# Causal attention layers: the scores of the first two query tiles in one step and one bank a head, and GpSimd's subtractions issued later

## The chip, the cores and the metric

The kernel runs on one core of a Trainium2 chip. The core has TensorE (PE in the profile; its weight loads are PEld), VectorE (DVE), ScalarE (ACT), GpSimd (POOL) and SyncE (SP), each with its own queue of instructions. The metric is the time of the whole program on the device in microseconds; lower is better.

## What is computed

Four layers work on x of shape (4, 512, 128) in float32: half a feed-forward part, attention, half a feed-forward part, each with a layer norm ahead and a residual. The change concerns the attention of layers 0 and 1, which are causal, with 16 heads of 8 values, 4 batches and 512 tokens. Cut to that:

```python
# layer 0, x normed
att = jnp.einsum('bhtd,bhsd->bhts', q, k) / np.sqrt(D) + bias      # bias: a table by head and distance
att = jnp.where(pos[None, :] > pos[:, None], -jnp.inf, att)
x = x + (softmax(att) @ v) @ proj_w.T + proj_b
# layer 1, x normed
logits = einsum(q1, k1) * einsum(q2, k2) * SCALE                   # ranks 4 and 8 a head
logits = jnp.where(causal, -jnp.inf, logits)
x = x + (softmax(logits) @ v) @ Wo.T + bo
```

The attention of layer 3 isn't causal and takes another branch of the same function; layer 2 has a recurrence instead.

## The kernel before

`attention()` (L566) serves layers 0, 1 and 3. A unit is one batch and one group of four heads, so a layer has 16 units. Queries are cut into four tiles of 128 rows, i = 0 to 3; tile i sees (i + 1) x 128 keys. The argument `added` (a table for layer 0, a mask for layer 1) selects the causal branch. Its names in the profile are `s_a` (scores), `sc_a` and `top_a` (scores with the addend, and each row's largest), `t_a` (transposed), `w_a` (weights by key), `acc_a` (their products with the values), `ou_a`, `ot_a`, `otok_a`, `oT_a` and `proj_a` (the output's way out).

For tile i of unit u the work is:

- `scores(u, i)`: TensorE makes four products, one a head, each in a PSUM bank of its own (L587). VectorE reduces them in the order of heads 2, 0, 3, 1: it adds the table or mask, writes the sum to SBUF and finds the row's largest (L604 for heads 0 and 1, L608 for 2 and 3). For heads 0 and 1 GpSimd subtracts the largest (L605), issued at once. For heads 2 and 3 ScalarE will take the exponential with the largest as its bias; this is kept in the list `put_off`.
- `exponentials()`: issues what is in `put_off` (L617) and empties it.
- `weights(u, i)`: TensorE transposes the scores by 128x128 blocks into banks (L628). ScalarE takes them out, with an exponential for heads 0 and 1 (L637) and a plain copy for heads 2 and 3 (L639).
- `values_up_to(u, i)`: TensorE multiplies by the padded values, all tiles and heads of a unit in one bank (L650). Behind tile 3, ScalarE copies the bank out (`summed`, L734).

The order of the instructions is written out by hand: within `manual_schedule` TensorE, VectorE, ScalarE and GpSimd run in the order in which the code issues. Banks come from a pool of eight and are handed on in the order of release, so which engine frees a new bank depends on the order too.

The main loop goes over u, and within u over j = 0 to 3. Each j issues: `weights(u, j)`; `exponentials()`; the values of the tile before (of unit u-1's tile 3 if j is 0); `scores(u + 1, j)`; then parts of other work, a step of the next batch's beginning (`begin_next`, with norm, transposition T_a at L180, then qk, or the factors in layer 1, and the values) or a step of what follows a finished batch (`go_on`). At j = 0 it also issues `start(u + 2)`: the unit's q on ScalarE in layer 0 (L911), q on VectorE and k on GpSimd in layer 1 (L1183), and two units into a batch the projection of the batch before (`ended`, L762). At j = 2 the unit before is normalized (`ot_a`, L741). A batch's norm has two steps on GpSimd (rs and rstd, L157 and L158), and its n is made on VectorE (L171) and then transposed and copied to `nT_a` (L127 on VectorE or L129 on ScalarE).

So a unit on TensorE is: t0, values of tile 3 of the unit before, s0, parts; t1, values of tile 0, s1, parts; t2, values of tile 1, s2, ot; t3, values of tile 2, s3. Here ti are the transposes of tile i of unit u and si the scores of tile i of unit u+1.

Of the kernel before, what the change touches and what calls it, by code (L numbers as in the profile page):

```python
# [11 lines left out]
AF = mybir.ActivationFunctionType  # L12
ALU = mybir.AluOpType
# [4 lines left out]
P = 128  # L18
# [3 lines left out]
NT = S // P  # L22
# [5 lines left out]
SLOT = 32  # L28
# [8 lines left out]
HUGE = 3.0e38  # L37
# [4 lines left out]
def kernel(ctx: ExitStack, tc: tile.TileContext, a: dict, out: bass.AP):  # L42
    nc = tc.nc
# [12 lines left out]
    def bank(name):  # L56
        return psum.tile([P, 512], FP, name=name, tag="bank", bufs=8)
# [508 lines left out]
    def attention(pool, tag, begin, project, residual, owT, added, after=None, beside=(), fetch=None):  # L566
# [5 lines left out]
        units = [(b, g) for b in range(NB) for g in range(NG)]  # L572
        st = {}

        def begun(b):
            if ("begin", b) not in st:
                st["begin", b] = begin(b)
            return next(st["begin", b], "end") != "end"

        def start(u):  # L580
            b, g = units[u]
            if g == 0:
                st["o", b] = pool.tile([P, NT, NG, NG * HD], FP, name=f"otok_{tag}{b}", tag="otok")
            st["qk", u] = project(b, g)

        def product(ps, q, k, r, i, n0, n1):
            nc.tensor.matmul(  # L587
                ps[:, n0:n1], q[r : r + SLOT, i * P : (i + 1) * P], k[r : r + SLOT, n0:n1], start=True, stop=True
            )


        def scores(u, i):
            b, g = units[u]
            q, k = st["qk", u]
            n = (i + 1) * P
            banks = [bank(f"s_{tag}{u}_{i}{r}") for r in range(4)]
            for r in range(4):
                product(banks[r], q, k, r * SLOT, i, 0, n)
            for r in (2, 0, 3, 1):
                sc = pool.tile([P, n], FP, name=f"sc_{tag}{u}_{i}{r}", tag=f"sc{i}", bufs=4)  # L600
                top = small.tile([P, 1], FP, name=f"top_{tag}{u}_{i}{r}", tag="top", bufs=16)
                more = added(g * 4 + r)[:, S - n :]
                if r < 2:
                    nc.vector.tensor_tensor_reduce(sc, banks[r][:, :n], more, 1.0, -HUGE, ALU.add, ALU.max, top)  # L604
                    nc.gpsimd.tensor_scalar(sc, sc, top, None, ALU.subtract)  # L605
                else:

                    nc.vector.tensor_tensor_reduce(sc, banks[r][:, :n], more, -1.0, HUGE, ALU.add, ALU.min, top)  # L608
                    put_off.append((sc, top))
                st["sc", u, i, r] = sc  # L610

        put_off = []

        def exponentials():

            for sc, top in put_off:
                nc.scalar.activation(sc, sc, AF.Exp, bias=top, scale=-1.0)  # L617
            put_off.clear()

        def weights(u, i):  # L620

            n = (i + 1) * P
            each = min(4, S // n)
            for r0 in range(0, 4, each):
                ps = bank(f"t_{tag}{u}_{i}{r0}")
                for x in range(each):
                    for j in range(i + 1):
                        nc.tensor.transpose(  # L628
                            ps[:, x * n + j * P : x * n + (j + 1) * P],
                            st["sc", u, i, r0 + x][:, j * P : (j + 1) * P],  # L630
                            ident,
                        )
                w = pool.tile([P, S], FP, name=f"w_{tag}{u}_{i}{r0}", tag="w", bufs=8)

                m = max(0, min(each, 2 - r0)) * n
                if m > 0:
                    nc.scalar.activation(w[:, :m], ps[:, :m], AF.Exp)  # L637
                if m < each * n:
                    nc.scalar.copy(w[:, m : each * n], ps[:, m : each * n])  # L639
                for x in range(each):  # L640
                    st["w", u, i, r0 + x] = w[:, x * n : (x + 1) * n]

        def values_up_to(u, i):

            b, g = units[u]
            if i == 0:
                st["acc", u] = bank(f"acc_{tag}{u}")
            for j in range(i + 1):
                for r in range(4):
                    nc.tensor.matmul(  # L650
                        st["acc", u][r * SLOT : (r + 1) * SLOT, i * P : (i + 1) * P],
                        vpads[b % 2][:, j, g * 4 + r, :],
                        st["w", u, i, r][:, j * P : (j + 1) * P],
                        start=(j == 0),
                        stop=(j == i),
                    )
            if i == NT - 1:
                summed(u)
# [15 lines left out]
        def lowered(u):  # L674
            q, k = st["qk", u]
            ps = bank(f"low_{tag}{u}")
            for i in range(NT):
                nc.tensor.transpose(ps[:, i * P : (i + 1) * P], st["low", u][:, i, :], ident)  # L678
            ql = pool.tile([P, S], FP, name=f"ql_{tag}{u}", tag="ql", bufs=2)
            nc.vector.tensor_tensor(ql, ps, q, ALU.add)  # L680
            st["ql", u] = ql
# [50 lines left out]
        def summed(u):  # L732
            o_u = pool.tile([P, S], FP, name=f"ou_{tag}{u}", tag="ou", bufs=3)
            nc.scalar.copy(o_u, st["acc", u])  # L734
            st["ou", u] = o_u
# [35 lines left out]
        def begin_next(u, between=False):  # L771
# [2 lines left out]
            b = (u + 1) // NG + 1  # L774
            return u % NG not in ((2, 3) if between else (2,)) and b < NB and begun(b)

        n_units = len(units)
        lead = 2 * NT + 2
        padded_values(pool)
# [7 lines left out]
        with tc.manual_schedule(engines={E_.PE, E_.DVE, E_.Activation, E_.Pool}):  # L787
            while begun(0):
                pass
            for u in range(3):  # L790
                if fetch is not None:
                    fetch(*units[u])
                if u > 0:
                    start(u - 1)
            if added:
                for i in range(NT):
                    scores(0, i)
                    exponentials()
            else:

                for n in range(0, lead, 2):
                    if n == 2 * NT:
                        lowered(0)
                    together(step(largest, n), step(largest, n + 1))
            for u in range(n_units + 1):
                last = u - 1
                now, nxt = u < n_units, u + 1 < n_units
                for j in range(NT):
                    n = 2 * (u * NT + j)

                    of = (u, j - 1) if j > 0 and now else (last, NT - 1) if j == 0 and last >= 0 else None
                    if added:
                        if now:
                            weights(u, j)
                        exponentials()

                        if of:
                            values_up_to(*of)
                        if nxt:
                            scores(u + 1, j)  # L820
                        if rest or not begin_next(u, True):
                            go_on()
                    else:
                        together(step(largest, n + lead), step(by_key, n))
                        if of:
                            times_values(*of, 0)
                        if j == NT - 1 and nxt:
                            lowered(u + 1)
                        if rest or not begin_next(u, True):
                            go_on()  # L830
                        together(step(largest, n + 1 + lead), step(by_key, n + 1))
                        if of:
                            times_values(*of, 1)
                    if j == 0 and u + 2 < n_units:
                        start(u + 2)
                    if j == 0 and last >= 1 and units[last - 1][1] == NG - 1:
                        ended(units[last - 1][0])
                    elif not begin_next(u):
                        go_on()
                    if j % 2:  # L840
                        next(beside, None)
                    if j == 2 and last >= 0:
                        normalized(last)
                    if j == 3 and fetch is not None and u + 3 < n_units:
                        fetch(*units[u + 3])
                    if j == 3 and last >= 0 and units[last][1] == NG - 1:
                        gathered(units[last][0])
            ended(NB - 1)
            while rest:
                go_on()  # L850
# [584 lines left out]
    ps = bank("gate0T")  # L1435
# [99 lines left out]
```

## Time and profile before

| | us |
|---|---|
| median of three runs | 1565.0 |
| the runs | 1563.73 to 1570.41 |
| profiled execution | 1562.17 |
| its span, first to last instruction | 1560.5 |
| causal attention of layer 0, about | 127 to 352 |
| causal attention of layer 1, about | 543 to 775 |

The mean granted clock of TensorE is 0.893 of full speed. The page's groups that the change touches (line, engine, operation, count, then busy time and mean ns of one, then the idle time ahead of them and what ended most of it):

```profile
L605 POOL TENSOR_SCALAR sc_a<-sc_a,top_a 128x128 f32<-128x128 f32 (+3 forms) x256 | 275.4, 1091 | 112.1 <-DVE top_a L604 72.2
L587 PE MATMUL s_a<-k_a,q_a 32*128 32x512 f32 (+3 forms) x1536 | 267.1, 549 | 17.9 <-DMA k_a<-fac_a 14.2
L628 PE MATMUL t_a<-ident,sc_a 128*128 128x128 f32 x1280 | 172.3, 282 | 6.0 <-DVE top_a L608 5.6
L617 ACT ACTIVATE sc_a<-sc_a,top_a 128x128 f32<-128x128 f32 (+3 forms) x256 | 135.0, 577 | 23.8 <-DVE top_a L608 23.6
L650 PE MATMUL acc_a<-w_a,vpad 128*32 128x128 f32 x2560 | 98.4, 280 | 0.6 <-DVE top_a L604 0.6
```

The group of L587 holds the products of layer 3 with those of the two causal layers. Busy times of TensorE overlap, since its matmuls are pipelined; for what a group costs in a row of groups, the distance from its start to the next group's start is the better measure.

### The profile page before, as it was taken

To read this page: it belongs to the slowest core of one execution; us is meant where nothing else is said; L and a number is where in the kernel's file an instruction comes from. 1 tells how busy PE (TensorE), PEld (TensorE's weight loads), DVE (VectorE), ACT (ScalarE), POOL (GpSimd) and SP (SyncE) were. 2 spreads that over 40 slices of the span, in tenths; PEclk is the share of its full clock that TensorE was granted. 3 is DMA by queue.
4 is the path that set the end of the run, shared out by engine and by line. 5 is a ranking of instruction groups with operands and counts; after the bars stand their busy time and mean duration, and the time that the engine had idled before them with its cause. 6 is when DMAs were issued, how large, how long until landed. Compare 5 with 4: busy or idle time off the path is not lost. (4 is left out here: it accounts for less than half of the span.)

```text
span 1560.5 us, 28691 instructions
## 1 busy us (share of the span) xinstructions
PE 1264.9 (81%) x10523; PEld 821.3 (53%) x10523; DVE 864.1 (55%) x2947; ACT 712.9 (46%) x1487; POOL 655.7 (42%) x789
## 2 busy tenths in 40 slices
PE   4777998995969688989988676718779999998394
PEld 3455676773756455766756655616533343333273
DVE  5335676773325365766556455515367787774343
ACT  1234876871443165768643322203325655564041
POOL 3455767872520176777501111273632214212253
PEclk9997999996979888999999778758979999999597
DMA  7420240002515474442033302214204000000223
GB/s 231 129 57 8 77 164 12 9 13 64 148 35 109 126 226 123 136 123 69 2 78 116 135 0 109 114 50 114 64 21 171 14 3 13 12 5 15 75 79 105
DMA packets 103092, 123.12 MB, mean 79 GB/s; under 512 B 9404, under 2 KB 74152, under 8 KB 100904
## 3 DMA queue, kind: packets, MB, share of 16 engines
q1 hardware_dynamic: 96296, 108.07, 23.2%
q0 software_dynamic: 6656, 13.22, 2.6%
q8 instruction: 84, 1.38, 0.4%
q14 instruction: 56, 0.46, 0.1%
HBM read 79.27 MB, written 41.98 MB: 78 GB/s over the span
## 5 line engine op out<-in xcount | busy, mean ns | idle before, releaser
L605 POOL TENSOR_SCALAR sc_a<-sc_a,top_a 128x128 f32<-128x128 f32 (+3 forms) x256 | 275.4, 1091 | 112.1 <-DVE top_a L604 72.2
L587 PE MATMUL s_a<-k_a,q_a 32*128 32x512 f32 (+3 forms) x1536 | 267.1, 549 | 17.9 <-DMA k_a<-fac_a 14.2
L692 ACT ACTIVATE w_a<-t_a 128x512 f32<-128x512 f32 x256 | 140.4, 595 | 119.7 <-PE t_a L587 94.8
L628 PE MATMUL t_a<-ident,sc_a 128*128 128x128 f32 x1280 | 172.3, 282 | 6.0 <-DVE top_a L608 5.6
L489 POOL DMA_INDIRECT res_f<-y_f,back_f x112 | 109.7, 980 | 141.8 <-ACT y_f L488 101.3
L587 PE MATMUL t_a<-ql_a,k_a 32*128 32x512 f32 x512 | 168.8, 643 | 0.5 <-DVE low_a__12599 L672 0.2
L628 PEld LDWEIGHTS t_a<-ident,sc_a 128*128 128x128 f32 x1280 | 145.1, 144 | 36.8 <-issue 13.8
L617 ACT ACTIVATE sc_a<-sc_a,top_a 128x128 f32<-128x128 f32 (+3 forms) x256 | 135.0, 577 | 23.8 <-DVE top_a L608 23.6
L587 PEld LDWEIGHTS s_a<-k_a,q_a 32*128 32x128 f32 x1536 | 93.7, 188 | 88.9 <-issue 43.1
L637 ACT ACTIVATE w_a<-t_a 128x256 f32<-128x256 f32 (+2 forms) x192 | 94.2, 526 | 64.2 <-PE t_a L628 63.7
L395 POOL DMA_INDIRECT disp_f<-n_f,to_f x96 | 94.3, 983 | 66.8 <-issue 58.8
L501 PE MATMUL o_f<-w_l,h_f 128*128 128x128 f32 (+1 forms) x896 | 113.0, 279 | 3.8 <-DVE o_f L483 3.3
L501 PEld LDWEIGHTS o_f<-w_l,h_f 128*128 128x128 f32 (+1 forms) x896 | 103.0, 184 | 14.7 <-DVE o_f L483 6.0
L466 PE MATMUL h_f<-dT_f,w_l 128*128 128x320 f32 (+1 forms) x256 | 107.8, 559 | 2.8 <-ACT dT_f L444 2.8
L157 POOL TENSOR_SCALAR rs_f<-mv_f 128x4 f32<-128x4 f32 (+1 forms) x23 | 6.5, 281 | 233.4 <-DVE mv_f L154 232.7
L650 PE MATMUL acc_a<-w_a,vpad 128*32 128x128 f32 x2560 | 98.4, 280 | 0.6 <-DVE top_a L604 0.6
L639 ACT COPY w_a<-t_a 128x256 f32<-128x256 f32 (+2 forms) x192 | 93.7, 528 | 6.7 <-PE t_a L628 6.5
L672 DVE TENSOR_REDUCE low_a__12599<-s_a 128x1 f32<-128x512 f32 x128 | 82.1, 685 | 26.3 <-PE t_a L587 18.5
L608 DVE CUSTOM_DVE_ANT_0 sc_a<-s_a,future 128x128 f32<-128x128 f32 (+3 forms) x128 | 62.3, 487 | 57.2 <-PE s_a L587 44.2
L672 DVE TENSOR_REDUCE low_a__12597<-s_a 128x1 f32<-128x512 f32 x128 | 81.3, 683 | 20.5 <-PE t_a L587 15.1
L608 DVE CUSTOM_DVE_ANT_0 sc_a<-s_a,table 128x128 f32<-128x128 f32 (+3 forms) x128 | 62.4, 487 | 53.0 <-PE s_a L587 52.5
L488 ACT ACTIVATE y_f<-o_f,d_f 128x128 f32<-128x128 f32 (+1 forms) x112 | 38.8, 394 | 105.9 <-DVE o_f L483 102.3
(337 smaller groups left out, 2260.8 us busy)
## 6 DMA issues: line engine op xcount, KB each, us to landing
gb_f<-rows_f SPq DMA_DIRECT2D x16, 1024.0 KB
fac_a<-fac_a_sb SPq DMA_DIRECT2D x36, 256.0 KB
disp_f<-zeros_f SPq DMA_DIRECT2D x4, 2080.0 KB
d_f<-disp_f SPq DMA_DIRECT2D x32, 260.0 KB
w_l<-in_L_ffn_w_dram SPq DMA_DIRECT2D x16, 512.0 KB
cb_f<-rows_f SPq DMA_DIRECT2D x16, 512.0 KB
q_a<-fac_a SPq DMA_DIRECT2D x32, 256.0 KB
k_a<-fac_a SPq DMA_DIRECT2D x32, 256.0 KB
```

Source lines behind the costliest of these rows:

```text
L395: nc.gpsimd.indirect_dma_start(out=self.to[c][i0 + t][:, :], out_offset=bass.IndirectOffsetOnAxis(ap=to[:, c, t : t + 1], axis=0), in_=ns[ ...
L466: nc.tensor.matmul(ps[u][:, :cap], w1[:, e, (c + u) * P : (c + u + 1) * P], dT, start=True, stop=True)
L489: nc.gpsimd.indirect_dma_start(out=self.back[e * per + s][:, :], out_offset=bass.IndirectOffsetOnAxis(ap=back[:m, s : s + 1], axis=0), in_ ...
L501: nc.tensor.matmul(po[:m, s, :], h[:, c, s * P : s * P + m], w2[:, e, c, :], start=(c == 0), stop=(c == NC - 1),)
L587: nc.tensor.matmul(ps[:, n0:n1], q[r : r + SLOT, i * P : (i + 1) * P], k[r : r + SLOT, n0:n1], start=True, stop=True)
L605: nc.gpsimd.tensor_scalar(sc, sc, top, None, ALU.subtract)
L608: nc.vector.tensor_tensor_reduce(sc, banks[r][:, :n], more, -1.0, HUGE, ALU.add, ALU.min, top)
L617: nc.scalar.activation(sc, sc, AF.Exp, bias=top, scale=-1.0)
L628: nc.tensor.transpose(ps[:, x * n + j * P : x * n + (j + 1) * P], st["sc", u, i, r0 + x][:, j * P : (j + 1) * P], ident,)
L650: nc.tensor.matmul(st["acc", u][r * SLOT : (r + 1) * SLOT, i * P : (i + 1) * P], vpads[b % 2][:, j, g * 4 + r, :], st["w", u, i, r][:, j * ...
L672: nc.vector.tensor_reduce(st["low", u][:, i, c : c + 1], ps, AX.X, ALU.max, negate=True)
L692: nc.scalar.activation(w, ps, AF.Exp)
```

## The change

`scores()` takes a tuple of tiles. A head's bank holds the scores of all tiles of the tuple side by side: for (0, 1), tile 0 in columns 0 to 127 and tile 1 in 128 to 383. All products of the tuple are issued first, then the reductions tile by tile, which are now in `larger()`. The main loop takes the tiles in steps (0, 1), (2,) and (3,), each at the j of its first tile: at j = 0 the weights of tiles 0 and 1, the values of the unit before's tile 3, and the scores of tiles 0 and 1; at j = 1 nothing of these; at j = 2 the weights of tile 2, the values of tiles 0 and 1 and the scores of tile 2; j = 3 as before. Parts, `start(u + 2)`, the projection and the normalization keep their j.

GpSimd's subtractions go into `put_off` with the exponentials, and both are issued by the next `exponentials()`, which runs at each j. Those of tiles 0 and 1 are so issued at j = 1, behind the parts and `start(u + 2)` of j = 0; those of tile 2 at j = 3, behind the parts of j = 2; those of tile 3 at the next unit's j = 0, behind its transposes' issue and the parts of j = 3. The exponentials of tile 0 move from the start of j = 1 to the same place with tile 1's behind them, and tile 1's move ahead from j = 2 to j = 1. The number of instructions of each kind and shape stays.

```diff
-        def scores(u, i):
+        def scores(u, tiles):
+
             b, g = units[u]
             q, k = st["qk", u]
+            banks = [bank(f"s_{tag}{u}_{tiles[0]}{r}") for r in range(4)]
+            at = {i: sum((x + 1) * P for x in tiles if x < i) for i in tiles}
+            for i in tiles:
+                for r in range(4):
+                    product(banks[r][:, at[i] :], q, k, r * SLOT, i, 0, (i + 1) * P)
+            for i in tiles:
+                larger(u, i, [ps[:, at[i] : at[i] + (i + 1) * P] for ps in banks])
+
+        def larger(u, i, banks):
+            b, g = units[u]
             n = (i + 1) * P
-            banks = [bank(f"s_{tag}{u}_{i}{r}") for r in range(4)]
-            for r in range(4):
-                product(banks[r], q, k, r * SLOT, i, 0, n)
             for r in (2, 0, 3, 1):
...
                 if r < 2:
-                    nc.vector.tensor_tensor_reduce(sc, banks[r][:, :n], more, 1.0, -HUGE, ALU.add, ALU.max, top)
+                    nc.vector.tensor_tensor_reduce(sc, banks[r], more, 1.0, -HUGE, ALU.add, ALU.max, top)
+                    put_off.append((sc, top, True))
+                else:
+
+                    nc.vector.tensor_tensor_reduce(sc, banks[r], more, -1.0, HUGE, ALU.add, ALU.min, top)
+                    put_off.append((sc, top, False))
+                st["sc", u, i, r] = sc
+
+        put_off = []
+
+        def exponentials():
+
+
+            for sc, top, less in put_off:
+                if less:
                     nc.gpsimd.tensor_scalar(sc, sc, top, None, ALU.subtract)
                 else:
...
+                    nc.scalar.activation(sc, sc, AF.Exp, bias=top, scale=-1.0)
             put_off.clear()
...
+        steps = ((0, 1), (2,), (3,))
...
-                for i in range(NT):
-                    scores(0, i)
+                for tiles in steps:
+                    scores(0, tiles)
                     exponentials()
...
+                        tiles = next((t for t in steps if t[0] == j), ())
                         if now:
-                            weights(u, j)
+                            for i in tiles:
+                                weights(u, i)
                         exponentials()
 
-                        if of:
-                            values_up_to(*of)
-                        if nxt:
-                            scores(u + 1, j)
+                        for i in steps[steps.index(tiles) - 1] if tiles else ():
+                            if j > 0 and now:
+                                values_up_to(u, i)
+                            elif j == 0 and last >= 0:
+                                values_up_to(last, i)
+                        if nxt and tiles:
+                            scores(u + 1, tiles)
                         if rest or not begin_next(u, True):
                             go_on()
```

More of the change, by code (lines that the diff above doesn't have):

```diff
@@ L603, in scores @@
                 if r < 2:
-                    nc.vector.tensor_tensor_reduce(sc, banks[r][:, :n], more, 1.0, -HUGE, ALU.add, ALU.max, top)
-                    nc.gpsimd.tensor_scalar(sc, sc, top, None, ALU.subtract)
-                else:
-                    nc.vector.tensor_tensor_reduce(sc, banks[r][:, :n], more, -1.0, HUGE, ALU.add, ALU.min, top)
-                    put_off.append((sc, top))
+                    nc.vector.tensor_tensor_reduce(sc, banks[r], more, 1.0, -HUGE, ALU.add, ALU.max, top)
+                    put_off.append((sc, top, True))
+                else:
+                    nc.vector.tensor_tensor_reduce(sc, banks[r], more, -1.0, HUGE, ALU.add, ALU.min, top)
+                    put_off.append((sc, top, False))
                 st["sc", u, i, r] = sc
@@ L614, in exponentials @@
         def exponentials():
-            for sc, top in put_off:
-                nc.scalar.activation(sc, sc, AF.Exp, bias=top, scale=-1.0)
+            for sc, top, less in put_off:
+                if less:
+                    nc.gpsimd.tensor_scalar(sc, sc, top, None, ALU.subtract)
+                else:
+                    nc.scalar.activation(sc, sc, AF.Exp, bias=top, scale=-1.0)
             put_off.clear()
```

## The prediction, made before the changed kernel ran

> **What bounds the kernel now.** I read the page's busy shares first, then the busy time of the engines in stretches of the two causal stages (about 127 to 352 us for L0, 543 to 775 us for L1), then TensorE's waits there, then the order of single groups.
>
> The page, whole program, busy time:
>
> ```profile
> PE 1264.9 (81%) x10523; PEld 821.3 (53%) x10523; DVE 864.1 (55%) x2947; ACT 712.9 (46%) x1487; POOL 655.7 (42%) x789
> ```
>
> The stretches (start:end, length, then busy us of PE, PEld, DVE, ACT, POOL, then the granted clock):
>
> ```profile
> 127.00:180.00 53.00, 47.27 (x544) 33.00 (x544) 34.01 (x155) 37.35 (x81) 36.19 (x36) 0.94 0.11 36
> 180.00:240.00 60.00, 56.67 (x712) 40.41 (x712) 45.77 (x205) 45.90 (x102) 43.27 (x46) 1.00 0.34 126
> 240.00:300.00 60.00, 54.98 (x668) 39.78 (x668) 41.18 (x184) 42.13 (x92) 42.57 (x45) 0.94 0.03 8
> 600.00:660.00 60.00, 57.43 (x730) 39.38 (x729) 42.60 (x181) 43.68 (x96) 44.66 (x42) 0.97 0.39 120
> ```
>
> TensorE is busy 89 to 96%, VectorE, ScalarE and GpSimd each 64 to 77%. So TensorE paces; the other three have 2.6 to 4 us of slack in a unit of 11.5, enough to be late at one place but not to bound the stage. TensorE's waits (total, times, longest), first from 127 to 360 us, then from 540 to 775 us:
>
> ```profile
> PE T_a L180 <- DVE n_a L171: 11.6, 6, 3.4
> PE proj_a L762 <- ACT ou_a L734: 1.6, 2, 0.8
> PE lg_f L322 <- DVE nT_f L127: 0.8, 1, 0.8
> ```
>
> ```profile
> PE s_a L587 <- DMA k_a<-fac_a: 14.2, 1, 14.2
> PE t_a L628 <- DVE top_a L608: 5.6, 5, 4.3
> PE T_a L180 <- DVE n_a L171: 5.4, 3, 3.7
> PE s_a L587 <- ACT w_a L637: 2.4, 1, 2.4
> ```
>
> Waits are few. What can be won is TensorE's own steps, and these few. One plain unit on TensorE (start, length, group):
>
> ```profile
> 164.96 0.66 PE L628 MATMUL t_a<-ident,sc_a 128*128 128x128 f32 x4
> 165.55 1.08 PE L650 MATMUL acc_a<-w_a,vpad 128*32 128x128 f32 x32
> 166.56 0.54 PE L587 MATMUL s_a<-k_a,q_a 32*128 32x128 f32 x8
> 167.02 1.09 PE L628 MATMUL t_a<-ident,sc_a 128*128 128x128 f32 x8
> 168.04 0.43 PE L650 MATMUL acc_a<-w_a,vpad 128*32 128x128 f32 x8
> 168.40 0.76 PE L587 MATMUL s_a<-k_a,q_a 32*128 32x256 f32 x8
> 169.09 1.82 PE L628 MATMUL t_a<-ident,sc_a 128*128 128x128 f32 x12
> 170.84 0.65 PE L650 MATMUL acc_a<-w_a,vpad 128*32 128x128 f32 x16
> 171.41 0.93 PE L587 MATMUL s_a<-k_a,q_a 32*128 32x384 f32 x8
> ```
>
> Start to start: t0 0.59, values of tile 3 1.01, s0 0.46, t1 1.02, values of tile 0 0.36, s1 0.69, t2 1.75, values of tile 1 0.57. With tile 3 behind, the unit ends at 176.47: 11.5 us.
>
> **What the Trainium skill says.** "PSUM — Partial Sum Buffer", section "PSUM bank collisions raise a hardware error": two engines must not touch one bank and quadrant at once, even in other columns, so semaphores guard whole banks. The changed program keeps this: VectorE's first reduction of tile 0 waits for a count that TensorE raises only behind tile 1's product in that bank. No trace here has two tiles in one bank yet. "TensorE: Matmul & The Clock Gate", Part 1, "What's actually happening": after an idle window of about 3.4 us the clock is halved until TensorE was busy about as long. The trace agrees: after waits of 2.77 and 2.13 us at 139 to 145 us the clock of the next 5 us is 0.51 and the sixteen transposes of tile 3 take 3.55 us instead of 1.84. "Trainium Architecture — The Big Picture", "Inside one NeuronCore": each engine works through its own stream and meets the others only at semaphores; hence I follow each engine's order.
>
> **The change part by part.** Counts of instructions are equal; order and banks change. A unit is one batch and four heads; 32 in the two stages, 30 with a next unit's scores.
>
> (1) Merged groups. t0 and t1 1.61 us, as twelve transposes in a row 1.46 (t2 without a wait): I take 1.50. Values of tiles 0 and 1 0.93, as 24 in a row 0.80 (tile 2's step, 174.60 to 175.40): 0.80. s0 and s1 1.15; s2 moves the same columns in half the products in 0.86: 1.00, an estimate between. Sum 0.39; I take 0.35, 30 times: -10.5.
>
> (2) t2's fourth group of transposes now takes the bank of the last unit's values, freed by ScalarE, instead of one freed by VectorE's first reduction of s1. It shows as 1.75 instead of 1.46 three times in L0 and as waits of about 0.2 to 0.4 us in L1, 1.1 together: -2.0.
>
> (3) TensorE comes about 1.5 us later, with more work ahead, to what it waited for in units with extra parts: the projection (step of s0 1.53 instead of 0.45: 1.1, three times: 3.3), router logits (1.0 once, and three s2 of 1.44 instead of 0.86 while ScalarE is late with weights: 2.7), ranks (s1 1.57 instead of 0.67, twice: 1.8). -7.8. Bound from below: nothing goes where the part's own chain moves along too.
>
> (4) Differences behind parts. GpSimd (0.61, 0.92, 1.25, 1.58 us by tile) now takes a batch's rs and rstd ahead of differences. For L0's last batch the wait is
>
> ```profile
> 249.79 0.66 PE L180 MATMUL T_a<-ident,n_a 128*128 128x128 f32 x2 [3.40 <-DVE n_a L171]
> ```
>
> and rstd stood behind two tile-2 differences, 2.47 us: -2.0. In L1's second batch one less, -1.0. The first wait of L0 (4.9 us, at 138 to 145) is behind differences in both orders: 0. The opposite side: start(u+2) and, in L1, GpSimd's k_a product pass ahead of differences. These are used a unit later, and GpSimd has 2.6 us of slack in each: 0, up to +0.3 a unit.
>
> (5) L1's third unit: VectorE's q_a, waiting for a DMA, stood ahead of s1's reductions, and t2 waited
>
> ```profile
> 592.32 1.54 PE L628 MATMUL t_a<-ident,sc_a 128*128 128x128 f32 x6 [4.31 <-DVE top_a L608]
> ```
>
> Both tiles' reductions now precede q_a. But tile 2's reductions still follow it, and GpSimd's k_a (done at 593.68) goes ahead of tile 0 and 1 work: from 593.68 and the differences then in line I estimate t3 1.8 us late and the next t0 2.0. -0.5.
>
> (6) New: ScalarE has exponentials of tiles 0 and 1 in one row ahead of w of tile 2, which frees the bank of the last s2 product. From t0's start: w0 and w1 to 2.2, two tile-3 exponentials to 3.5, sums copy to 3.9, q_a (0.74, L0 only) to 4.7, four exponentials to 6.1, first w2 to 6.55. TensorE is there at 1.50+1.01+1.00+1.46+0.80+0.65=6.42. With the restart that is 0.33 us in about 12 units of L0: +4.0; in L1 there is no q_a on ScalarE, w2 comes at 5.8: 0. Bounds: 0 and 1.1 a unit.
>
> (7) New: VectorE starts about 0.5 us later for the whole bank, and values of tile 0 take the first of these banks: it is free 2.3 us after s0's start, TensorE wants it at 2.46. Semaphores make it 0 to 0.2; 0.07 over 30: +2.0.
>
> (8) New: parts of j=0 and j=1 stand back to back. In batches 2 and 3 the transposes of n are followed at once by qk (or the factors), and the copy to nT is behind 2.2 us of reductions (4 x 0.21 + 4 x 0.345) on VectorE. Four places of -0.35 to +1.0: +2.0. If each wait were over 2 us, the clock goes down too, which cost 1.7 us in the transposes at 145 us alone.
>
> Sum: -10.5-2.0-7.8-3.0-0.5+4.0+2.0+2.0=-15.8. From the profiled execution, 1562.2 us, 1546.4; the median of the runs shown, 1565.0, is 2.8 above it, so I shift it: 1549.
>
> **The rivals.** A, likeliest: as summed, 1549.
>
> B, all new waits hide: (6) to (8) at zero, -23.8: 1541. For it: 2.7 us of slack on ScalarE in each unit. Against: the row of 6.55 against 6.42.
>
> C, no change: the ScalarE row is late in all 30 units by 0.5 us (+15 in place of +4) and half of (3) isn't got, because ranks and logits move with their own chain (+3.9): -0.9, 1564. For it: half steps of 1.44 us in s2 have been seen three times as soon as ScalarE had 0.2 us more.
>
> D, slower: ScalarE's late w2. Its price would be 1.1 us a unit, 30 times, +33 in place of +4: +13, 1578. It decides from 0.66 us a unit, where 19.8 of gain is used up. For it: the one wait of s2 for w_a in L1, 2.4 us, was followed by a clock of 0.51 for 6 us. Against: ScalarE is only 70 to 77% busy, and what is late in j=0 is caught up by j=3, where TensorE has 3.7 us for tile 3.
>
> **How the numbers follow.** A 0.54, B 0.17, C 0.17, D 0.12. The measurement tells 0.5%, 7.8 us, from no change: faster is below 1557.2, slower above 1572.8. A lies under that but for 0.03, B wholly, C within, D above: faster 0.68, same 0.20, slower 0.12. The range: from a little under B, since (3) or (4) can be larger, 1535, to C with its own spread, 1567; D is left out. A's own range is 1541 to 1558.
>
> **What would show it.** In a plain unit t, t, values 3, then eight s products of 1.0 us, with the next t0 10.9 to 11.3 us on instead of 11.5. Right for (3): no gap before the projection at the ends of batches. Right for (6): s2 of 1.2 to 1.4 us in L0 with ScalarE's w_a as releaser, and 0.86 in L1. Right for (4): the wait for n_a of the last L0 batch under 1.5 us. Wrong: plain units of 11.5 or more; new waits of 1 us or more of t for GpSimd or VectorE; a clock below 0.94 in the stretches shown. The other stages (full attention of L3, the feed-forward stages) should stand within 1 us.

## The result and the profile after

| | before | changed |
|---|---|---|
| median of ten runs, us | 1566.32 | 1560.01 |
| range, us | 1563.73 to 1570.41 | 1553.19 to 1565.41 |
| ratio, with 95% interval | | 0.9957 [0.9945, 0.9969] |
| profiled execution: span, us | 1560.5 | 1555.8 |
| L0, first score product to last `ot`, us | 226.1 | 222.2 |
| L1, the same stretch, us | 229.8 | 227.0 |

The change gains 6.3 us, 0.43%, where 15.8 were forecast. The two attention stages together give 6.7 us less in the profile, so the gain is where it was looked for and its size is wrong; the rest of the program is 2.0 us longer. The 1560.0 lies in the forecast range of 1535 to 1567, but above likeliest case A's own, 1541 to 1558. (A line number of L612 and above in the changed kernel is moved: the reductions are L612 and L616, transposes L640, values L662, ScalarE's first weights L649, GpSimd's subtractions L627.)

The page's first part, after:

```profile
PE 1261.2 (81%) x10523; PEld 825.9 (53%) x10523; DVE 863.6 (56%) x2947; ACT 712.9 (46%) x1487; POOL 659.6 (42%) x789
```

The counts are as before and the busy times within 1%: this is a matter of order alone. The stretches of time, after (start:end, length, busy us of PE, PEld, DVE, ACT and POOL, clock):

```profile
180.00:240.00 60.00, 56.46 (x721) 41.21 (x716) 44.89 (x205) 44.49 (x99) 42.80 (x44) 0.94 0.38 135
240.00:300.00 60.00, 56.78 (x705) 41.49 (x706) 44.05 (x198) 44.44 (x99) 45.45 (x47) 0.94 0.04 11
600.00:660.00 60.00, 56.11 (x686) 40.44 (x688) 42.31 (x180) 42.99 (x95) 48.06 (x47) 0.97 0.40 120
```

TensorE is as busy as before, so the shares don't tell what went wrong. TensorE's order in a plain unit does (start, length, group; L1). Before, from t2 to `ot`:

```profile
648.97 1.53 PE L628 MATMUL t_a<-ident,sc_a 128*128 128x128 f32 x12
650.43 0.65 PE L650 MATMUL acc_a<-w_a,vpad 128*32 128x128 f32 x16
651.00 0.93 PE L587 MATMUL s_a<-k_a,q_a 32*128 32x384 f32 x8
651.86 0.66 PE L741 MATMUL ot_a<-ident,ou_a 128*128 128x128 f32 x4
```

After, from t0 and t1 in one row to `ot`:

```profile
721.65 1.53 PE L640 MATMUL t_a<-ident,sc_a 128*128 128x128 f32 x12
723.11 1.08 PE L662 MATMUL acc_a<-w_a,vpad 128*32 128x128 f32 x32
724.12 0.94 PE L587 MATMUL s_a<-k_a,q_a 32*128 32x128 f32 x16
724.99 1.53 PE L640 MATMUL t_a<-ident,sc_a 128*128 128x128 f32 x12
726.58 0.86 PE L662 MATMUL acc_a<-w_a,vpad 128*32 128x128 f32 x24
727.38 1.72 PE L587 MATMUL s_a<-k_a,q_a 32*128 32x384 f32 x8
729.03 0.66 PE L753 MATMUL ot_a<-ident,ou_a 128*128 128x128 f32 x4
```

Start to start, the merged groups are 1.46, 0.87 and 0.80, together 0.56 less than the six they replace (1.61, 1.15, 0.93). That is more than forecast. But s2 now takes 1.65 instead of 0.86 and t2 1.59 instead of 1.46, and a plain unit is 11.57 us, against 11.2 (L1) and 11.5 (L0) before. No idle time is printed for s2, because a waiting product hides behind its three neighbours. The weight loads show it (start, length, group, idle time ahead and what ended it):

```profile
726.58 0.59 PEld L662 LDWEIGHTS acc_a<-w_a,vpad 128*32 128x32 f32 x24 [0.30 <-DVE top_a L616]
727.38 0.53 PEld L587 LDWEIGHTS s_a<-k_a,q_a 32*128 32x128 f32 x6 [0.20 <-DVE top_a L616]
728.19 0.29 PEld L587 LDWEIGHTS s_a<-k_a,q_a 32*128 32x128 f32 x2 [0.28 <-ACT w_a L649]
```

Three heads load at 727.38, the fourth at 728.19, when ScalarE has taken out the first transposes of tile 2, whose bank it gets. The loads of the values ahead of it wait a little too, 0.30 us for VectorE's maxima where 0.17 stands in units without that wait; this is t2's 0.13. ScalarE's queue then:

```profile
725.13 0.60 ACT L746 COPY ou_a<-acc_a 128x512 f32<-128x512 f32 x1
725.60 0.81 ACT L629 ACTIVATE sc_a<-sc_a,top_a 128x128 f32<-128x128 f32 x2
726.56 0.51 ACT L629 ACTIVATE sc_a<-sc_a,top_a 128x256 f32<-128x256 f32 x1 [0.15 <-DVE top_a L616]
727.25 0.51 ACT L629 ACTIVATE sc_a<-sc_a,top_a 128x256 f32<-128x256 f32 x1 [0.18 <-DVE top_a L616]
727.67 0.85 ACT L649 ACTIVATE w_a<-t_a 128x384 f32<-128x384 f32 x2
```

The weights of tile 2, wanted at once, stand behind the exponentials of tiles 0 and 1, wanted a unit later; and these wait for VectorE's maxima. The first weights start at 727.67, 2.68 us after the first transpose of t2; where nothing stands ahead of them (e3 below) it is 0.64.

The second place is the beginning of a batch. L0's third batch, after:

```profile
192.06 0.94 PE L587 MATMUL s_a<-k_a,q_a 32*128 32x128 f32 x16
193.02 0.49 PE L180 MATMUL T_a<-ident,n_a 128*128 128x128 f32 x2
195.93 0.69 PE L180 MATMUL T_a<-ident,n_a 128*128 128x128 f32 x2 [2.42 <-DVE n_a L171]
197.40 3.78 PE L920 MATMUL qk_a<-nT_a,wmixed_l 128*128 128x512 f32 x4 [0.78 <-DVE nT_a L127]
200.98 1.54 PE L876 MATMUL v_a<-wqkvT_l,nT_a 128*128 128x128 f32 x8
```

VectorE in that time (its short readings of the maxima are left out):

```profile
193.79 0.29 DVE L612 CUSTOM_DVE_ANT_0 sc_a<-s_a,table 128x128 f32<-128x128 f32 x1
...
195.04 0.42 DVE L612 CUSTOM_DVE_ANT_0 sc_a<-s_a,table 128x256 f32<-128x256 f32 x1
...
195.38 0.60 DVE L171 TENSOR_SCALAR n_a<-x,mv_a,rstd_a 128x128 f32<-128x128 f32 x2
196.66 0.69 DVE L127 COPY nT_a<-T_a 128x512 f32<-128x512 f32 x1 [0.68 <-PE T_a L180]
```

The second half of n follows all eight reductions, and TensorE has nothing to do in between. The clock falls with it; windows of the same place, after:

```profile
192.00:198.00 6.00, 2.77 (x28) 1.61 (x22) 4.65 (x23) 3.66 (x8) 6.00 (x7) 0.76 0.01 3
198.00:204.00 6.00, 6.00 (x33) 3.86 (x34) 1.44 (x2) 1.75 (x4) 1.48 (x2) 0.67 0.00 0
```

qk's four products span 3.78 us at that clock. Before, in the same place, they spanned 1.98 at full clock:

```profile
191.53 0.41 PE L180 MATMUL T_a<-ident,n_a 128*128 128x128 f32 x2 [1.43 <-DVE n_a L171]
193.01 0.44 PE L180 MATMUL T_a<-ident,n_a 128*128 128x128 f32 x2 [1.07 <-DVE n_a L171]
195.25 1.98 PE L901 MATMUL qk_a<-nT_a,wmixed_l 128*128 128x512 f32 x4
```

That was in part chance. In a later profile of the kernel before (e6 below), with waits of 1.44 and 1.07 there, the clock fell as well:

```profile
194.00:200.00 6.00, 6.00 (x37) 3.59 (x37) 2.79 (x10) 2.35 (x6) 3.04 (x3) 0.73 0.00 0
195.89 2.60 PE L901 MATMUL qk_a<-nT_a,wmixed_l 128*128 128x512 f32 x4
```

From `ot` to `ot`, by kind of unit, in the two profiled executions:

| units | before | after | difference |
|---|---|---|---|
| nine plain ones | 103.4 | 104.9 | +1.5 |
| five with a projection | 66.4 | 60.8 | -5.5 |
| five with router logits or ranks (L0) | 65.6 | 62.1 | -3.5 |
| four that begin batch 3 or 4 | 74.7 | 80.3 | +5.6 |
| L1's first full one (the DMA wait of step 5) | 17.7 | 14.0 | -3.7 |
| L1, two around 690 us | 30.4 | 28.7 | -1.7 |

The first rows of the two stages and their ends add +0.4. In the four beginnings the printed waits for n and nT sum to 10.6 us before and 11.2 after, so most of their +5.6 isn't in printed waits. Much of it goes with the clock (qk above), and between the two later profiles (e6 and e5 below) it is only +0.6.

### The profile page after: what moved, and what is told of

Its sections match the earlier page's. It is cut to its first block, busy times and chain, and to the rows that moved or that the text cites. A ratio compares the mean times of both kernels' runs of the same rounds, so it can differ in the third digit from the quotient of the medians.

```text
span 1555.8 us, 28669 instructions
## 1 busy us (share of the span) xinstructions
PE 1261.2 (81%) x10523; PEld 825.9 (53%) x10523; DVE 863.6 (56%) x2947; ACT 712.9 (46%) x1487; POOL 659.6 (42%) x789
## 5 line engine op out<-in xcount | busy, mean ns | idle before, releaser
L627 POOL TENSOR_SCALAR sc_a<-sc_a,top_a 128x128 f32<-128x128 f32 (+3 forms) x256 | 277.7, 1100 | 98.8 <-DVE top_a L612 85.2
L640 PE MATMUL t_a<-ident,sc_a 128*128 128x128 f32 x1280 | 163.3, 278 | 2.2 <-DVE otok_a L757 1.2
L640 PEld LDWEIGHTS t_a<-ident,sc_a 128*128 128x128 f32 x1280 | 143.8, 143 | 25.9 <-POOL sc_a L627 11.8
L395 POOL DMA_INDIRECT disp_f<-n_f,to_f x96 | 94.9, 988 | 66.4 <-issue 58.6
L649 ACT ACTIVATE w_a<-t_a 128x256 f32<-128x256 f32 (+2 forms) x192 | 94.5, 525 | 61.9 <-PE t_a L640 61.7
L616 DVE CUSTOM_DVE_ANT_0 sc_a<-s_a,future 128x128 f32<-128x128 f32 (+3 forms) x128 | 62.5, 488 | 55.6 <-PE s_a L587 43.8
L662 PE MATMUL acc_a<-w_a,vpad 128*32 128x128 f32 x2560 | 90.9, 278 | 1.5 <-DVE top_a L616 0.9
L616 DVE CUSTOM_DVE_ANT_0 sc_a<-s_a,table 128x128 f32<-128x128 f32 (+3 forms) x128 | 62.4, 487 | 43.9 <-PE s_a L587 38.0
```

The costliest lines, as they stand in the source:

```text
L395: nc.gpsimd.indirect_dma_start(out=self.to[c][i0 + t][:, :], out_offset=bass.IndirectOffsetOnAxis(ap=to[:, c, t : t + 1], axis=0), in_=ns[ ...
L616: nc.vector.tensor_tensor_reduce(sc, banks[r], more, -1.0, HUGE, ALU.add, ALU.min, top)
L640: nc.tensor.transpose(ps[:, x * n + j * P : x * n + (j + 1) * P], st["sc", u, i, r0 + x][:, j * P : (j + 1) * P], ident,)
```

## The experiments

The theory: TensorE's merged groups win, and two queues give it back, ScalarE's at s2 and VectorE's at the beginnings of batches. The rivals: GpSimd's late subtractions cost it; VectorE's late release of the banks does; or the beginnings are bound by the norm's own chain. The experiments ran on other chips than the first comparison. There the kernel before takes 1583.6 to 1587.0 us, so only ratios to it are compared; each is from five rounds. "Stages" is the sum of the two stretches of the first table; for the kernel before and the changed kernel profiled among these runs they are 461.9 and 454.7.

**Each half alone.** In the changed kernel:

```diff
-        steps = ((0, 1), (2,), (3,))
+        steps = ((0,), (1,), (2,), (3,))
```

> Only the subtractions put off, the four tiles in steps of their own. Main theory (the change wins on TensorE's merged groups and loses about 0.8 us at the fourth product of s2 in plain units, and 2 to 3 us in each batch beginning with its parts back to back): the late subtractions are nearly free and take 2 us from the beginning of L0's last batch; s2 stays at 0.86, plain units at 11.2 to 11.5; 0 to 5 us less than before, about 1563. Rival (the late subtractions cost what the merge won): slower than before by 6 us or more, with waits of the transposes for sc_a from GpSimd.

Ratio 0.9936 [0.9912, 0.9959], 10 us less; stages 454.0. The late subtractions cost nothing and win more than expected: the unit that begins L0's last batch takes 16.85 us, against 21.83 in the kernel before (e6). GpSimd has rstd ready 0.6 us after the start of tile 0's products there, 2.5 in e6. Both waits for n are shorter (2.16 and 0.96 in e6):

```profile
249.36 0.75 PE L180 MATMUL T_a<-ident,n_a 128*128 128x128 f32 x2 [1.09 <-DVE n_a L171]
251.00 0.44 PE L180 MATMUL T_a<-ident,n_a 128*128 128x128 f32 x2 [0.89 <-DVE n_a L171]
```

That is 1.1 of the 5.0 us. Most of the rest goes with the clock, which stays full here over the next 6 us and is 0.61 in e6.

The other half, with the subtractions issued at once:

```diff
-                    put_off.append((sc, top, True))
+                    nc.gpsimd.tensor_scalar(sc, sc, top, None, ALU.subtract)
```

> The merged step kept, the subtractions issued at once as before. Main theory: the two losses stay, so plain units stay at 11.6 and s2 at 1.66, and the time within 4 us of the changed kernel, about 1561. Rival (late subtractions are the loss): 6 us or more less than the changed kernel, 1554 or less, with s2 at 0.86 or the beginnings of batches without their waits.

Ratio 0.9926 [0.9903, 0.9949]; stages 451.9; s2 at 1.65 in plain units. So GpSimd's lateness isn't the loss. The same unit of L0's last batch takes 21.84 us here. The changed kernel again, on the next chip:

> The changed kernel itself, for comparison with its variants beside it. Main theory: its ratio to the kernel before stands at 0.994 to 0.996, so above both halves alone (0.9936 and 0.9926 measured), since both take the same waits away and the merge's two losses stay. Rival: on one chip it is 0.988 or less, the sum of the halves, and the smaller gain came from the chip.

Ratio 0.9945 [0.9930, 0.9959], within the intervals of each half alone: the halves do not add. In the changed kernel that unit takes 20.40: what the late subtractions free on GpSimd is in part taken by the eight reductions ahead of n's second half on VectorE, which TensorE awaits for 2.17 us, and the clock falls to 0.58. The kernel before against itself:

> The kernel before itself, for a profile beside its variants and as a gauge of the comparison: ratio 0.998 to 1.002 in every theory.

Ratio 1.0003 [0.9992, 1.0015].

**ScalarE's row.** The list is walked as before, but at j = 1 the exponentials stay in it, and j = 2 issues them behind its `weights`:

```diff
-        def exponentials():
+        def exponentials(later=False):
...
+                elif later:
+                    kept.append((sc, top, less))
...
-            put_off.clear()
+            put_off[:] = kept
...
-                        exponentials()
+                        exponentials(later=(j == 1))
```

> The changed kernel with ScalarE's exponentials of tiles 0 and 1 moved behind its work on the transposes of tile 2; all else as it was. Main theory: the bank of the fourth s2 product comes free 1 us earlier, s2 goes from 1.66 to 0.86 in all plain units (some 14 of them, and 3 to 5 smaller ones) and a plain unit from 11.57 to 10.8: 12 us less than the changed kernel, about 1548. Rival (s2 is late because VectorE frees its banks late, having started half a microsecond later): s2 stays above 1.4 and the time within 3 us of the changed kernel.

Ratio 0.9883 [0.9861, 0.9904]; stages 444.6. Against the changed kernel's 0.9945 that is 9.8 us. Under the kernel before it is 18.6 us; the forecast's sum without its term for ScalarE's row, (6), is 19.8. A plain unit of it, TensorE, in L1:

```profile
719.91 1.53 PE L642 MATMUL t_a<-ident,sc_a 128*128 128x128 f32 x12
721.37 1.08 PE L664 MATMUL acc_a<-w_a,vpad 128*32 128x128 f32 x32
722.38 0.94 PE L587 MATMUL s_a<-k_a,q_a 32*128 32x128 f32 x16
723.25 1.53 PE L642 MATMUL t_a<-ident,sc_a 128*128 128x128 f32 x12
724.71 0.86 PE L664 MATMUL acc_a<-w_a,vpad 128*32 128x128 f32 x24
725.50 0.93 PE L587 MATMUL s_a<-k_a,q_a 32*128 32x384 f32 x8
726.36 0.66 PE L755 MATMUL ot_a<-ident,ou_a 128*128 128x128 f32 x4
```

s2 is 0.86, t2 is 1.46, and the unit 10.64 us. VectorE's start and its order are untouched, so its later start on a shared bank isn't what held s2. In L0 plain units take 10.98: t2 is 1.80 there, since the values now wait for ScalarE's w_a, and three s2 of units with logits stay at 1.15.

**The beginnings of batches.** Here the parts of j = 1 are issued behind tile 2's transposes, the first part of j = 0 ahead of tile 0's reductions, and tile 1's reductions at j = 1:

```diff
+                        if j == 1:
+                            reductions()
                         if now:
                             for i in tiles:
                                 weights(u, i)
+                        if j == 2:
+                            if rest or not begin_next(u, True):
+                                go_on()
+                            if not begin_next(u):
+                                go_on()
+                            next(beside, None)
...
-                        if rest or not begin_next(u, True):
+                        if j > 1:
+                            reductions()
+                        if j != 1 and (rest or not begin_next(u, True)):
                             go_on()
+                        if j == 0 and reduce_later:
+                            larger(*reduce_later.pop(0))
```

> The changed kernel with the parts of j=1 moved behind the transposes of tile 2, the first part of j=0 ahead of tile 0's reductions, and tile 1's reductions behind the parts of j=0. ScalarE's order is as in the changed kernel, so that tile 1's exponentials come a little later still. Main theory: the waits for nT of 0.8 and 2.5 to 2.6 us in the beginnings of batches fall below 0.5 and TensorE's clock stays up there, 2 to 3 us each in four to five places, while s2 stays at 1.66 or gets worse by up to 0.5 in plain units: 0 to 10 us less than the changed kernel. Rival (the beginnings are bound by GpSimd's rstd and VectorE's n, not by where the parts stand): the same waits stand ahead of T_a or the factors, and no unit with a beginning is shorter.

Ratio 0.9952 [0.9934, 0.9971]: no net gain over the changed kernel. Both halves of the expectation showed. The units that begin batches 3 and 4 fell to 14.42 and 15.55 in L0 and to 15.72 twice in L1, from 19.2 to 20.4 in the changed kernel (e5). Most plain ones rose to 12.2, and in L1 nine waits of the values for tile 1's late reductions sum to 8.5 us. With ScalarE's order of e3 added:

> Parts apart as in e4 and ScalarE's exponentials of tiles 0 and 1 behind tile 2's weights as in e3. Main theory: plain units near 11 (tile 1's late reductions hold the bank that the values of tile 0 wait for, which cost 0.6 us a unit in e4), units with a beginning 14.5 to 16 instead of 19.5 to 20.5: 3 to 9 us under e3 if the first stays small, ratio 0.982 to 0.988. Rival (beginnings are bound elsewhere): not below e3's 0.988.

Ratio 0.9819 [0.9803, 0.9834]; stages 432.2. Plain units are 10.7 to 11.3 in the main, beginnings 14.7 to 15.9. The two mends help each other. Then only where it is due: e3 with a like order in every fourth unit, and as in the changed kernel elsewhere. `scores` now stops ahead of each tile's reductions, so that the first part of j = 0 stands ahead of tile 0's and the second ahead of tile 1's; parts of j = 1 follow tile 2's transposes.

```diff
+                        begins = u % NG == 0
...
-                            scores(u + 1, tiles)
+                            reduced = scores(u + 1, tiles)
+                            next(reduced)
+                            if begins and j == 0:
+                                if rest or not begin_next(u, True):
+                                    go_on()
+                                next(reduced)
+                                if not begin_next(u):
+                                    go_on()
+                            for _ in reduced:
+                                pass
```

> As e3, and only in units that begin a batch (every fourth) the first part stands ahead of tile 0's reductions, the second between tile 0's and tile 1's, and those of j=1 behind tile 2's transposes. Main theory: plain units 10.6 to 11.0 as in e3 and beginnings 15 to 16.5 instead of 19.5 to 21: 10 to 16 us under e3, ratio 0.978 to 0.983, the best so far. Rival: as for e7, at 0.988.

Ratio 0.9786 [0.9761, 0.9810]; stages 425.0. This beats both kernels: 34 us under the kernel before, 25 under the changed one. The beginning of L0's third batch in it:

```profile
188.72 0.94 PE L587 MATMUL s_a<-k_a,q_a 32*128 32x128 f32 x16
189.59 0.44 PE L180 MATMUL T_a<-ident,n_a 128*128 128x128 f32 x2
190.27 0.58 PE L180 MATMUL T_a<-ident,n_a 128*128 128x128 f32 x2 [0.24 <-DVE n_a L171]
190.69 1.68 PE L644 MATMUL t_a<-ident,sc_a 128*128 128x128 f32 x12
192.21 1.88 PE L946 MATMUL qk_a<-nT_a,wmixed_l 128*128 128x512 f32 x4
```

The wait for n is 0.24 instead of 2.42, there is none for nT, and qk runs at full speed.

**Are the two losses one?** e8 with `exponentials()` back at j = 1, so the changed kernel with its beginnings mended only:

> As e8, with ScalarE's exponentials of tiles 0 and 1 back ahead of tile 2's weights, so the changed kernel with only its beginnings mended. If the two losses are apart from each other: beginnings 15 to 17 us, plain units 11.6 with s2 at 1.66, 14 to 17 us less than the changed kernel, ratio 0.984 to 0.987. Rival (they share a cause, such as the clock): beginnings above 18, ratio 0.989 to 0.995.

Ratio 0.9830 [0.9809, 0.9852], 18 us under the changed kernel; beginnings 14.72, 14.92 and 16.11 twice, plain units 11.57, s2 still 1.65 (the distance to `ot`):

```profile
715.60 1.72 PE L587 MATMUL s_a<-k_a,q_a 32*128 32x384 f32 x8
717.25 0.66 PE L757 MATMUL ot_a<-ident,ou_a 128*128 128x128 f32 x4
```

They are apart: e3 takes one away, this run the other.

**Are the late subtractions still needed?** e8 with the edit of e2:

> As e8, with the subtractions issued at once. If putting them off still helps in the mended kernel (rs and rstd of a batch ahead of them on GpSimd): 0 to 8 us over e8, ratio 0.979 to 0.984, with the beginnings longer by the wait for n. Rival (they only add lateness once the parts stand apart, as the merge alone at 0.9926 beside both at 0.9945 suggests): ratio 0.974 to 0.978.

Ratio 0.9790 [0.9769, 0.9810], not to be told from e8. L0's last beginning is 19.25 us instead of 15.71, while two units of L1 are 1.2 and 2.0 shorter; stages 425.8. The expectation's two cases stay undecided.

**Was the beginning a loss before the change too?** The kernel before, with the first part of j = 0 ahead of tile 0's reductions in every fourth unit:

```diff
+            if first is not None:
+                first()
             for r in (2, 0, 3, 1):
```

> The kernel before, with one thing changed: in every fourth unit the first part of j=0 (the second half of n) stands ahead of tile 0's reductions on VectorE. If the beginnings were bound by VectorE's order before as well: 0.5 to 2 us less in each of four, ratio 0.995 to 0.999. Rival (there GpSimd's rstd binds, late behind subtractions): tile 0's reductions now wait for it too and the ratio is 1.000 to 1.005.

Ratio 0.9969 [0.9959, 0.9979], 5 us less. In the profile 2.1 of it shows in L0, where the stretch is 229.7 instead of 231.8 us and the beginnings are 0.7 and 1.0 shorter; L1's stretch is no shorter, and where the rest lies isn't shown. VectorE's order held up the kernel before too. So the beginnings are only in part a loss of the change: the four take 78.6 us in the kernel before (e6), 79.2 in the changed one (e5) and 61.9 in e10. Most of what e10 wins is time that the kernel before spent there too.

## Why the prediction was right and wrong

- **What bounds it.** Right. TensorE paces, and most of every gain lies in its steps of the two stages, but for e11. The forecast's own sign of being wrong came: plain units of 11.5 or more.
- **(1), merged groups.** Too small: 0.56 in place of 0.39 a unit, s0 and s1 together 0.87 and not 1.00.
- **(2), t2.** Right: the waits of t2's transposes for VectorE that it counted are gone, but for one of 0.25 us in the unit of (5). (Those in L1 summed to 1.3, not 1.1.) That t2 is 1.59 in most plain units is the wait of (7).
- **(3), waits of units with other parts.** Right in the main. The table's -9.0 for these ten units holds the merged groups of (1) too. By steps, three projections give 1.1 each, logits 1.0 once and ranks 0.9 twice, but the three s2 of units with logits, 1.44 before, are still 1.26 to 1.50: about -6.4, an estimate from these steps, where -7.8 was put. The merge brings it: e2 has it (12.0 for a projection unit of L0, as after) and e1 has not (12.5 to 13.6).
- **(4), rstd ahead of subtractions.** The mechanism is right in L0's last batch: alone (e1) it makes that unit 5.0 us shorter, though most of this goes with the clock. In the changed kernel the unit is 0.6 to 1.4 shorter, and the wait for n, forecast under 1.5 us, is 2.15, because the reductions of two tiles now precede n's second half. The -1.0 in L1's second batch didn't come: the wait for n there is 3.71 us, before 3.67, and rs itself waits 1.46 us for VectorE's mv_a.
- **(5).** More than forecast: -3.7 in that unit, of which 0.56 are merged groups, where -0.5 was put. And 593.68, read as the end of GpSimd's k_a, is its start in that trace; it ends at 594.95.
- **(6), ScalarE's row: this step failed.** It had TensorE wanting the bank "at 1.50+1.01+1.00+1.46+0.80+0.65=6.42" and the weights at 6.55. For L0 the weights came as computed: the fourth product starts 6.54 after t0 in a plain unit there, and also in the L1 unit shown, 728.19 - 721.65. But TensorE is there at 727.38, 5.73 after t0 (5.73 in L0 too). The term of 0.65 for three products ahead is wrong, since the four heads' products run beside each other and all are wanted at the start of s2. So the wait is 0.81, and as the late product has no neighbours left, all of it is added to s2. And "in L1 there is no q_a on ScalarE, w2 comes at 5.8: 0" is wrong: L1 has the same 0.8, because the exponentials wait for VectorE's maxima there: the row of four takes 2.07 us from start to start, 1.45 in L0. In place of 0.33 in 12 units stand 0.8 in 14 and 0.3 to 0.4 in three (and the three s2 with logits named at (3)), about 12 us by the lengths of s2. Moving the exponentials (e3) wins 9.8 us net, where the whole step was put at 4.0.
- **(7).** Right, and near in size: printed waits of values for reductions are 0.9 us in all, but in the weight loads, where t2's 0.13 shows, they sum to 2.4 us over 14 units, beyond the 0.17 that stands without a wait; 2.0 were put.
- **(8), parts back to back.** The mechanism is right, the size too small: with (4) the four beginnings were to stay level, and they lost 5.6 us in the first profiles, though only 0.6 among the later ones. In L1 the named wait, for nT, grew from 1.06 to 2.54 and 2.60 while the one for n went. In L0 the second wait for n was left out. The clock's fall was named but not counted; as it can come to the kernel before as well, how much of the 5.6 belongs to the change stays open.

So of the rivals, D's mechanism, ScalarE's late w2, acted with its price at 0.8 a unit in half the units, not 1.1 in all. C's outcome, 1564, was nearer than A's, in part by luck: its +15 for ScalarE's row is near the 12 above, but half of (3), which it gave up, mostly came.

## What to carry to other kernels

When groups on the pacing engine are merged, ask of each other engine's queue which item is wanted first, and put work for the next round behind work for this one: here two such reorderings are worth 25 us on top of the changed kernel's 9, though the larger gain lies in a place that was slow before the change too. Where several small products run beside each other, the bank of the last is wanted when the first starts. And what once lay between two dependent steps has to be put back: T_a and qk need the transposes of tile 2 between them.

## What had not been expected of the hardware

A product of s2 is two instructions of about 0.53 us each, yet four heads' products end 0.86 us after the first starts. The Trainium skill says so ("TensorE: Matmul & The Clock Gate", Part 3, "The mechanism": products at different tile positions run at the same time); the reading of before had the number and didn't use it.

The same page's Part 1, "What's actually happening", has the clock fall after an idle window of about 3.4 us. Here less was enough: waits of 2.42 and 0.78 us with 0.7 us of work between left 0.67 of the clock over the next 6 us. The waits of 2.77 and 2.13 us in which the prediction saw the page confirmed are each shorter too. With 1.43 and 1.07 in the same place the kernel before kept full clock in its first profile, and with 1.44 and 1.07 in a later one (e6) it fell to 0.73. So these runs show no length of wait that decides.
